# Out-projection with 128 tokens per matmul, and attention weights kept on chip, in a four-layer scan and attention kernel

## The chip, the cores and the metric

The kernel runs on one core of a Trainium2 chip. The metric is the device time of one execution in microseconds (us), the median of the runs shown. The core has five instruction streams that run beside each other and wait for each other by semaphores: PE (matrix products), DVE and POOL (elementwise work), ACT (elementwise functions and copies) and SP. SP here only issues DMA transfers, all of them, from one queue in order.

## What is computed

The input `x` is 4 images of 64 x 64 tokens with 96 channels. Four layers follow each other:

- layer 0 is a selective-scan block on the normalized image. Tokens are projected to an inner width (192), convolved with a 3 x 3 depthwise filter, scanned in four directions with 16 states per channel (`h = h * exp(dt * A) + dt * u * B`, `y = sum(h * C)`), normalized, multiplied by a gate `silu(z)`, projected back to 96 channels and added to `x`;
- layer 1 does the same in the frequency domain: a real two-dimensional FFT gives 33 x 64 frequencies, real and imaginary parts make 192 channels, the inner width is 384, and after the out-projection (384 to 192 channels) the inverse FFT is added to its input;
- layers 2 and 3 are an attention without softmax, whose value for all tokens can be had from one small product `x^T x`, and a feed-forward network quantized to 8-bit floats.

```
y = _layernorm(y, out_norm_w, out_norm_b)
y = y * jax.nn.silu(z)
return y @ out_proj_w.T        # layer 1: [64 x 33 tokens, 384] @ [384, 192]
```

## The kernel before

**Stages.** `build` runs a head, a long scan stage and a tail. The head (`alone(head, begin0, 0)`) normalizes and projects the first two images of layer 0 with nothing beside it; the task is `normalized` and then `Block.project`. The scan stage (`scans`) goes through six phases: two for layer 0 (two images each) and four for layer 1 (one image each). The tail (`alone(tail, end1, 3)`) finishes image 3: out-projection, inverse FFT, layers 2 and 3.

**Scan steps.** A phase takes four directions, each cut into segments of tokens (eight of 512 for layer 0; 512, 512, 384, 384 and 320 for layer 1). A segment has 12 steps: four quarters of the 16 states times three groups of 128 channels. So there are 2 x 384 + 4 x 240 = 1728 steps. In a step, ACT makes the decay factors (L682), PE transposes the inputs into PSUM (L678), DVE runs four scans (L710), POOL makes the other inputs (L700) and multiplies by C (L747), and PE adds up over the states (L757). The broadcast rows of B and C come by DMA (L624), B and C of a quarter being fetched about three steps ahead into two buffers each.

**Side tasks.** What isn't scan work is written as Python generators that are stepped from three places in every scan step (`slot`). `RATES` gives how many yields of the side tasks a step may take: 2.82 in the layer 1 phases. A yield can ask for a certain place (`LATE`, `BURST`). The side tasks queue up over phases: the phases of images 1, 2 and 3 are given `end1` of images 0, 1 and 2, and `begin1` (FFT, input projection and gate) of all images comes before. When a side task ends, the next one starts; after the last one the remaining scan steps have nothing beside them. In the scan stage the order on PE, DVE, ACT and POOL is the order in which the program is written out, while that of SP's transfers comes from the planner of the framework, as does that of all engines in head and tail. With `E.wide` over 1 (head and tail) up to three such workers are interleaved.

**`end1`, where most of the edit lies.** `Block.gated` goes over the rows of frequencies in blocks of 8, 8, 6, 6 and 5 rows of 64 tokens (in the tail three workers: blocks 0 and 3, 1 and 4, and 2). It loads the scan outputs (`yt`, L403 and L407; `ut`, L409) and the gate (`zb`, L423), transposes and sums them, normalizes, applies the gate (L481 in the tail) and calls the out-projection `out1`. That takes one row of 64 tokens per matmul: `y[:, c, ...]` (128 channels x 64 tokens) is the stationary operand, `wo[:, c, :]` (128 x 192) the moving one, three channel groups are summed in PSUM (L1019), two rows go to ACT in one copy (L1026), and one transfer per block stores them in `att` (L1028), which lies as [64, 33, 192] in DRAM. An f32 matmul shows as two instructions.

`inverse` then loads `ih`, `iw` (L1098, L1100) and `att` in three channel groups of 32 (`at`, L1106), and does two sets of matmuls (L1117, L1133). `tokens` runs layers 2 and 3. It loads the attention weights of a layer with `weights` (L1207): in the scan stage those of layer 2 at its start and those of layer 3 when it comes to it; in the tail those of both layers, and `end1` takes its first yield (`next(rest)`) ahead of `inverse`, so that these eight loads stand ahead of `inverse`'s own on SP. The feed-forward weights are quantized once, in the side task `quantized` of the first phase, and kept.

**Inputs of the projections.** The class `Inputs` prefetches the weights `wi` (L145) and the token tiles `xi` (L150) for `project` (half 0) and `gate` (half 1). `wi` holds both halves, of which `in_proj` (L210) uses one.

Of the kernel before, what the change touches and what calls it, by code (L numbers as in the profile page):

```python
# [7 lines left out]
F32 = mybir.dt.float32  # L8
# [10 lines left out]
NB, HH, WW, CH = 4, 64, 64, 96  # L19
# [3 lines left out]
C, P = 3, 128  # L23
# [7 lines left out]
class Cfg:  # L31
# [5 lines left out]
    def __init__(self, pre, NI, KI, NR, nat, R, parts, rows, segs, eps):  # L37
        self.pre = pre
        self.NI, self.PI, self.KI = NI, P // NI, KI
        self.DI = C * self.PI  # L40
        self.NR, self.L, self.nat = NR, NR * 64, nat
        self.R, self.M = R, R + 2 * NST
        self.parts = parts
        self.rows = [(sum(rows[:i]), n) for i, n in enumerate(rows)]
        self.segs = [(sum(segs[:i]), n) for i, n in enumerate(segs)]
        self.eps = eps
# [66 lines left out]
def together(tasks, width):  # L113

    tasks, active = list(tasks), []
    while tasks or active:
        while tasks and len(active) < width:
            active.append(tasks.pop(0))
        for task in list(active):
            try:  # L120
                yield next(task)
            except StopIteration:
                active.remove(task)


class Inputs:


    def __init__(self, blk, sp, xf, chunks, half, nm, w):
        self.blk, self.sp, self.xf, self.half, self.nm, self.w = blk, sp, xf, half, nm, w  # L130
        self.todo = [
            (c, r, n) for c in chunks for p0, p1 in blk.cfg.parts for r, n in blk.rows_of(p0, p1, half == 0)
        ]
        self.ahead, self.wi = [], {}
        for _ in range(2):
            self.load()

    def load(self):
        if not self.todo:
            return  # L140
        sp, cfg, nc = self.sp, self.blk.cfg, self.blk.nc
        c, r, n = self.todo.pop(0)
        if c not in self.wi:
            t = sp.tile([CH, cfg.KI, 2, cfg.PI], F32, name=f"{cfg.pre}_wi_{self.nm}_{c}", tag=f"wi{self.w}", bufs=2)
            nc.sync.dma_start(out=t, in_=self.blk.w["inw"][:, :, :, c, :])  # L145
            self.wi[c] = t
        x = sp.tile(
            [CH, 2, 512], F32, name=f"xi{self.half}_{self.nm}_{c}_{len(self.todo)}", tag=f"xin{self.w}", bufs=3
        )
        nc.sync.dma_start(out=x[:, :, : n * 64], in_=self.xf[:, :, r * 64 : (r + n) * 64])  # L150
        self.ahead.append((self.wi[c], x))
# [6 lines left out]
class Block:  # L158


    def __init__(self, tc, pool, cfg, w, ident, dram):
# [4 lines left out]
        def load(name, shape, src=None):  # L166
            t = pool.tile(list(shape), F32, name=f"{cfg.pre}_{name}", tag=f"{cfg.pre}{name}")
            nc.sync.dma_start(out=t, in_=w[name] if src is None else src)
            return t

        self.xpw = load("xpw", (P, C, 4, cfg.NI * cfg.M))
        self.dtw = load("dtw", (cfg.NI * cfg.M, 4, C * P))
        self.dtb = load("dtb", (P, C, 4))
# [29 lines left out]
    def in_proj(self, out, wi, half, xin, n):  # L203

        cfg = self.cfg
        for i in range(cfg.NI):
            for ki in range(cfg.KI):
                if i or ki:
                    yield
                self.nc.tensor.matmul(  # L210
                    out[i * cfg.PI : (i + 1) * cfg.PI, :n],
                    wi[:, ki, half, :],
                    xin[:, max(i, ki), :n],
                    start=(ki == 0),
                    stop=(ki == cfg.KI - 1),
                )
# [789 lines left out]
def out1(att, b):  # L1006


    def task(E, blk, sp, wo, y, r, nr, w):
        nc = E.nc  # L1010
        a = sp.tile([HH, 8, 2 * CH], F32, name=f"ab_{b}_{r}", tag=f"ab{w}")
        for i0 in range(0, nr, 2):
            m = min(2, nr - i0)
            po = E.psum(f"po1_{b}_{r}_{i0}")[:HH, : 4 * CH].rearrange("p (k c) -> p k c", k=2)
            for i in range(m):
                if i:
                    yield
                for c in range(C):
                    nc.tensor.matmul(  # L1019
                        po[:, i, :],  # L1020
                        y[:, c, (i0 + i) * HH : (i0 + i + 1) * HH],
                        wo[:, c, :],
                        start=(c == 0),
                        stop=(c == C - 1),
                    )
            E.defer(lambda i0=i0, m=m, po=po: nc.scalar.copy(a[:, i0 : i0 + m, :], po[:, :m, :]))  # L1026
            yield
        nc.sync.dma_start(out=att[:, r : r + nr, :], in_=a[:, :nr, :])  # L1028

    return task  # L1030

# [124 lines left out]
def quantized(E, cp, ins, quant):  # L1156

    nc = E.nc
    shapes = (("w1", [CH, 4 * CH]), ("w2", [P, 3, CH]), ("b1", [P, 3]), ("b2", [P, CH]))
    with E.pool("qw") as sp:  # L1160
        loaded = []
        for ly in (2, 3):
            for name, shape in shapes:
                t = sp.tile(shape, F32, name=f"{name}_{ly}", tag=f"{name}{ly}")
                src = ins[f"l{ly}_{name}"]
                nc.sync.dma_start(out=t, in_=src.to_broadcast([P, CH]) if name == "b2" else src)
                loaded.append((ly, name, shape, t))
        for _ in range(6):
            yield
        for ly, name, shape, t in loaded:  # L1170
            keep = cp if name in ("w1", "w2") else sp
            r = keep.tile(shape, F8, name=f"q{name}_{ly}", tag=f"q{name}{ly}")
            yield LATE
            nc.vector.tensor_copy(r, t, saturate=False)
            if keep is sp:
                r, q = cp.tile(shape, F32, name=f"k{name}_{ly}", tag=f"k{name}{ly}"), r
                nc.vector.tensor_copy(r, q)
            quant[ly][name] = r
    yield


def tokens(E, ins, consts, ident, x1, b, out, quant):
# [4 lines left out]
    nc = E.nc  # L1187
    A, Q, W = CH + 1, 8, E.wide
    with E.pool(f"tk{b}") as sp:
# [7 lines left out]
            nc.scalar.copy(id16, ident)  # L1197
        nc.gpsimd.memset(xn[:, :, CH:A], 1.0)

        def weights(ly):  # L1200

            nm, w, bufs = f"{b}_{ly}", {}, min(W, 2)
            for name, shape in (
                ("wqkv", [A, 3 * CH]), ("wqt", [CH, A]), ("wff", [CH, CH]), ("bff", [A, CH]),
            ):
                t = w[name] = sp.tile(shape, F32, name=f"{name}_{nm}", tag=name, bufs=bufs)
                nc.sync.dma_start(out=t, in_=ins[f"l{ly}_{name}"])  # L1207
            w.update(quant[ly])
            return w

        ws = [weights(ly) for ly in ((2, 3) if W > 1 else (2,))]
        yield
        x = sp.tile([P, NT, CH], F32, name=f"tok_{b}", tag="tok")
        nc.sync.dma_start(out=x, in_=x1.rearrange("(p t) c -> p t c", t=NT))
# [71 lines left out]
        def small(rows, lhs, rhs, name, into):  # L1286

            pw = E.psum(name)[:rows, : rhs.shape[1]]
            nc.tensor.matmul(pw, lhs, rhs, start=True, stop=True)
            E.defer(lambda: into(pw))  # L1290
# [83 lines left out]
            yield from together([layer_norm(f"{b}_2a", p) for p in parts], W)  # L1374
        for ly in (2, 3):
            nm = f"{b}_{ly}"
            if len(ws) < ly - 1:
                ws.append(weights(3))
            q = ws[ly - 2]
            wq = q["wqkv"]  # L1380
            if W == 1:
                yield from norm_all(nm + "a")
            pg = E.psum(f"pg_{nm}")[:A, :A]
            for t in range(NT):
                nc.tensor.matmul(pg, xn[:, t, :], xn[:, t, :], start=(t == 0), stop=(t == NT - 1))  # L1385
                if t % 4 == 3:
                    yield
            gs = sp.tile([A, A], F32, name=f"gs_{nm}", tag="gs")
            nc.scalar.copy(gs, pg)
            yield  # L1390
            gv = sp.tile([A, CH], F32, name=f"gv_{nm}", tag="gv")
            small(A, gs, wq[:, 2 * CH : 3 * CH], f"pgv_{nm}", lambda t: nc.scalar.copy(gv, t))
            yield
            mt = sp.tile([CH, CH], F32, name=f"mt_{nm}", tag="mt")
            small(CH, gv, wq[:, CH : 2 * CH], f"pm_{nm}", lambda t: nc.vector.tensor_tensor(mt, t, mask, ALU.mult))
            yield
            pw = sp.tile([CH, CH], F32, name=f"pws_{nm}", tag="pws")
            small(CH, mt, q["wff"], f"pw_{nm}", lambda t: nc.scalar.copy(pw, t))
            yield
            wo = sp.tile([A, CH], F32, name=f"wo_{nm}", tag="wo")  # L1400
            small(A, q["wqt"], pw, f"pe_{nm}", lambda t: nc.vector.tensor_tensor(wo, t, q["bff"], ALU.add))
            yield
            if W > 1:
                yield from together([part(ly, p, wo, q) for p in parts], W)
                continue
            for g in range(NT // 4):
                yield from attend(nm, g, 0, wo)
            yield from norm_all(nm + "f")
            for g in range(NT // 4):
                yield from feed(nm, g, 0, q)  # L1410
# [212 lines left out]
```

## Time and profile before

| | |
|---|---|
| median of 3 runs | 11260.47 us (11260.01 to 11280.23) |
| the profiled execution | 11260.07 us |
| its span, first to last instruction | 11258.3 us |
| head (to the first L747) | 0 to 221.8 us |
| scan, layer 0 phases | 221.8 to 5135.5 us |
| scan, layer 1 phases | 5135.5 to some 10877 us, 1456, 1413, 1435 and 1434 us |
| tail | some 10877 to 11258.3 us |
| L1019, all images | 792 instructions, first at 7103.6, last at 11018.3 us |
| L1028, stores of `att` | 20, at 445 to 500 ns on SP's queue |
| L1207, attention weights | 8 loads of each of four names, 7548.9 to 11029.7 us |
| feed-forward of images 0, 1, 2 ended (their L1412 store) | 8307.7 us; some 9583; 10842.7 us |

An execution's time is 1.8 us above its span here, for what lies around it. In the lines of the timeline the first number is the start and the second the length, both in us; in brackets stands the time for which the engine sat idle before, and what ended that. SPq is SP's DMA queue: its time is that of issuing a transfer, not of moving the data. PEld are weight loads, which overlap PE's matmuls. An entry of PE stands for an instruction from start to end, so entries overlap, and the spacing of starts tells the rate.

### The profile page before, as it was taken

How to read it: one execution, taken by the hardware profiler on the slowest of the kernel's cores; microseconds unless marked ns; L12 is line 12 of the kernel's file. 1: busy time of each engine (PE TensorE's matmuls, PEld its weight loads, DVE VectorE, ACT ScalarE, POOL GpSimd, SP SyncE). 2: the span in 40 equal slices, each digit the busy share in tenths (PEclk: the TensorE clock that was granted, in tenths of full speed). 3: DMA queues.
4: the chain of work that ended last, by engine and by line, in shares of the span. 5: the costliest groups of instructions: out<-in, count | busy, mean ns of one | idle time of the engine just before them, and what ended most of it. 6: DMA issues, size and time to landing. Idle time of an engine off the chain costs nothing. (4 is left out here: it accounts for less than half of the span.)

```text
span 11258.3 us, 163664 instructions
## 1 busy us (share of the span) xinstructions
PE 9023.4 (80%) x54944; PEld 6618.2 (59%) x54944; DVE 9756.0 (87%) x10419; ACT 9354.2 (83%) x19456; POOL 9614.9 (85%) x7464
## 2 busy tenths in 40 slices
PE   6678788777888888888888888887788777887775
PEld 2555555555667666656665665655556555655554
DVE  6889999889999998999888787988988889789864
ACT  3779999998898998998778788879888888778853
POOL 2999999888998998999789798988989889889860
PEclk8889999888998998999889899998899888899887
DMA  4655554555665556555554444542244322542242
GB/s 146 146 131 128 133 131 120 153 158 143 163 162 134 137 138 144 133 144 161 154 141 131 128 135 137 172 118 92 96 138 143 102 92 98 157 125 96 82 131 40
DMA packets 1205139, 1466.87 MB, mean 130 GB/s; under 512 B 480839, under 2 KB 1017295, under 8 KB 1145799
## 3 DMA queue, kind: packets, MB, share of 16 engines
q1 hardware_dynamic: 1204295, 1456.40, 47.7%
q8 instruction: 434, 7.11, 0.3%
q14 instruction: 410, 3.36, 0.1%
HBM read 1219.66 MB, written 236.50 MB: 129 GB/s over the span
## 5 line engine op out<-in xcount | busy, mean ns | idle before, releaser
L747 POOL TENSOR_TENSOR h_l<-h_l,bc_l 128x1536 f32<-128x1536 f32 (+2 forms) x1728 | 4784.4, 2769 | 192.1 <-DVE h_l L710 73.1
L700 POOL TENSOR_TENSOR h_l<-du_l,bc_l 128x512 f32<-128x512 f32 (+2 forms) x3456 | 3970.4, 1172 | 620.1 <-PE acc_l L757 581.1
L646 ACT ACTIVATE bx_l<-dut_l,bt_l 128x192 f32<-128x192 f32 (+2 forms) x6272 | 2754.6, 499 | 0.3
L757 PE MATMUL acc_l<-ident,h_l 128*128 128x128 f32 (+1 forms) x16656 | 2430.6, 299 | 243.5 <-POOL h_l L747 242.1
L757 PEld LDWEIGHTS acc_l<-ident,h_l 128*128 128x128 f32 (+1 forms) x16656 | 2130.9, 154 | 836.8 <-POOL h_l L747 384.9
L682 ACT ACTIVATE ax_l<-delta_l,l_alog 128x512 f32<-128x512 f32 (+2 forms) x3456 | 2140.7, 667 | 0.0
L710 DVE TENSOR_TENSOR_SCAN h_l<-b_l,state_l,h_l 128x512 f32<-128x512 f32 (+2 forms) x1388 | 1507.6, 1109 | 123.1 <-ACT b_l L682 104.5
L678 PE MATMUL b_l<-ident,bx_l 128*128 128x128 f32 (+1 forms) x6886 | 1215.4, 295 | 210.2 <-DVE h_l L710 203.2
L678 PEld LDWEIGHTS b_l<-ident,bx_l 128*128 128x128 f32 (+1 forms) x6886 | 854.6, 149 | 816.6 <-DVE h_l L710 464.4
L682 ACT ACTIVATE b_l<-delta_l,l_alog 128x512 f32<-128x512 f32 (+2 forms) x1970 | 1232.6, 626 | 117.2 <-DVE h_l L710 49.4
L710 DVE TENSOR_TENSOR_SCAN b_l<-ax_l,state_l,b_l 128x512 f32<-128x512 f32 (+2 forms) x853 | 967.5, 1134 | 254.8 <-PE b_l L678 253.6
L678 PE MATMUL ab_l<-ident,bx_l 128*128 128x128 f32 x5312 | 896.1, 298 | 223.1 <-DVE h_l L710 213.2
L710 DVE TENSOR_TENSOR_SCAN h_l<-ab_l,state_l,h_l 128x512 f32<-128x512 f32 x803 | 992.7, 1261 | 83.2 <-ACT ab_l L682 48.8
L682 ACT ACTIVATE ab_l<-delta_l,l_alog 128x512 f32<-128x512 f32 x1326 | 912.8, 688 | 152.3 <-DVE h_l L710 81.4
L757 PE MATMUL acc_l<-ident,k_l 128*128 128x128 f32 x4760 | 785.8, 293 | 294.8 <-DVE k_l L728 281.6
L710 DVE TENSOR_TENSOR_SCAN h_l<-ax_l,state_l,b_l 128x512 f32<-128x512 f32 (+2 forms) x853 | 963.2, 1129 | 65.0 <-PE b_l L678 62.7
L678 PEld LDWEIGHTS ab_l<-ident,bx_l 128*128 128x128 f32 x5312 | 654.2, 151 | 583.4 <-DVE h_l L710 414.9
L728 DVE TENSOR_TENSOR k_l<-b_l,bc_l 128x512 f32<-128x512 f32 (+2 forms) x1344 | 832.2, 619 | 47.2 <-DMA bc_l<-l_xd_l 1.0
L297 PE MATMUL pc_l<-pad_l,l_dg 128*128 128x512 f32 (+2 forms) x1656 | 788.1, 564 | 59.5 <-ACT uh_l L275 46.8
L757 PE MATMUL acc_l<-ident,hk_l 128*128 128x128 f32 x3628 | 591.8, 297 | 293.7 <-DVE hk_l L728 280.8
L757 PEld LDWEIGHTS acc_l<-ident,k_l 128*128 128x128 f32 x4760 | 582.8, 150 | 390.7 <-DVE k_l L728 317.9
L710 DVE TENSOR_TENSOR_SCAN ab_l<-ax_l,state_l,ab_l 128x512 f32<-128x512 f32 x496 | 631.9, 1274 | 114.5 <-PE ab_l L678 113.8
(252 smaller groups left out, 14452.2 us busy)
## 6 DMA issues: line engine op xcount, KB each, us to landing
bc_l<-l_xd_l SPq DMA_DIRECT2D x640, 512.0 KB
bc_l<-l_xd_l SPq DMA_DIRECT2D x512, 256.0 KB
bc_l<-l_xd_l SPq DMA_DIRECT2D x128, 1024.0 KB
bc_l<-l_xd_l SPq DMA_DIRECT2D x128, 768.0 KB
us_l<-l_u SPq DMA_DIRECT2D x96, 768.0 KB
l_y<-y_l SPq DMA_DIRECT2D x288, 256.0 KB
yt_l<-l_y SPq DMA_DIRECT2D x264, 192.0 KB
yt_l<-l_y SPq DMA_DIRECT2D x128, 384.0 KB
```

The costliest lines, as they stand in the source:

```text
L297: nc.tensor.matmul(pc[:, : n * 64].rearrange("p (r w) -> p r w", w=64), diag[:, t, :], pad[:, r - p0 + dy : r - p0 + dy + n, dx : dx + 64] ...
L646: nc.scalar.activation(t[:n, b, :, ch], z.dut[:n, b, :, ch], AF.Copy, scale=z.bt[:n, b, m : m + 1])
L678: nc.tensor.transpose(pb[:, t : t + n], st.z.bx[st.q, j][:n, b, st.c], ident[:n, :n])
L682: nc.scalar.activation(out, z.delta[:, st.c, : z.S], AF.Exp, scale=z.blk.A[:, st.c, z.k, n : n + 1])
L700: nc.gpsimd.tensor_tensor(st.h[:, 1 + j, :S], st.z.du[:, st.c, :S], st.z.b[st.q][:, j, :S], ALU.mult)
L710: nc.vector.tensor_tensor_scan(h[:, ::step], a[:, ::step], b[:, ::step], 0.0 if z.first else z.state[st.c][:, n : n + 1], ALU.mult, ALU.add,)
L728: nc.vector.tensor_tensor(hk[:, : z.S], kept_at(st, j), z.c[st.q][:, j, : z.S], ALU.mult)
L747: nc.gpsimd.tensor_tensor(h, h, z.c[st.q][:, 1 : 1 + m, : z.S], ALU.mult)
L757: nc.tensor.matmul(z.acc[st.c][:m, b, :], hc[:, t : t + m], ident, start=(first and b == 0), stop=(last and b == 0), is_transpose=True,)
```

## The change

Four edits:

- `out1` takes pairs of rows, 128 tokens per matmul, so the result has 128 partitions: the even row of a pair in partitions 0 to 63, the odd one in 64 to 127. A block of 8, 6 or 5 rows makes 4, 3 or 3 tiles (the last of 5 with 64 tokens). One copy takes two tiles; a single row has a copy of its own. `att` gets two stores per block, one for the even and one for the odd rows, and a third where a row is single.
- The number of yields of `out1` goes with the tiles: 17 an image, where it was 33.
- The attention weights of layers 2 and 3 are loaded in `quantized` into the pool that lives as long as the program; `weights` and its loads go.
- `Inputs` loads the half of `wi` that is used, and makes `xin` tiles as long as its longest block.

```diff
@@ Inputs
-        self.ahead, self.wi = [], {}
+        self.ahead, self.wi, self.most = [], {}, 64 * max(n for _, _, n in self.todo)
...
-            t = sp.tile([CH, cfg.KI, 2, cfg.PI], F32, ..., tag=f"wi{self.w}", bufs=2)
-            nc.sync.dma_start(out=t, in_=self.blk.w["inw"][:, :, :, c, :])
+            t = sp.tile([CH, cfg.KI, cfg.PI], F32, ..., tag=f"wi{self.w}", bufs=2)
+            nc.sync.dma_start(out=t, in_=self.blk.w["inw"][:, :, self.half, c, :])
...
-            [CH, 2, 512], F32, ..., tag=f"xin{self.w}", bufs=3
+            [CH, 2, self.most], F32, ..., tag=f"xin{self.w}", bufs=3
@@ in_proj
-                    wi[:, ki, half, :],
+                    wi[:, ki, :],
@@ out1
-        a = sp.tile([HH, 8, 2 * CH], F32, name=f"ab_{b}_{r}", tag=f"ab{w}")
-        for i0 in range(0, nr, 2):
-            m = min(2, nr - i0)
-            po = E.psum(f"po1_{b}_{r}_{i0}")[:HH, : 4 * CH].rearrange("p (k c) -> p k c", k=2)
+        a = sp.tile([P, 4, 2 * CH], F32, name=f"ab_{b}_{r}", tag=f"ab{w}")
+        pairs = nr // 2
+        for i0 in range(0, (nr + 1) // 2, 2):
+            m = min(2, (nr + 1) // 2 - i0)
+            po = E.psum(f"po1_{b}_{r}_{i0}")[:, : 4 * CH].rearrange("p (k c) -> p k c", k=2)
             for i in range(m):
+                t, n = (i0 + i) * P, P if i0 + i < pairs else HH
                 if i:
                     yield
                 for c in range(C):
                     nc.tensor.matmul(
-                        po[:, i, :],
-                        y[:, c, (i0 + i) * HH : (i0 + i + 1) * HH],
-                        wo[:, c, :],
-                        start=(c == 0),
-                        stop=(c == C - 1),
+                        po[:n, i, :], y[:, c, t : t + n], wo[:, c, :], start=(c == 0), stop=(c == C - 1)
                     )
-            E.defer(lambda i0=i0, m=m, po=po: nc.scalar.copy(a[:, i0 : i0 + m, :], po[:, :m, :]))
-            yield
-        nc.sync.dma_start(out=att[:, r : r + nr, :], in_=a[:, :nr, :])
+
+            def put(i0=i0, m=m, po=po):
+                full = min(m, pairs - i0)
+                if full > 0:
+                    nc.scalar.copy(a[:, i0 : i0 + full, :], po[:, :full, :])
+                if full < m:
+                    nc.scalar.copy(a[:HH, pairs : pairs + 1, :], po[:HH, full : full + 1, :])
+
+            E.defer(put)
+            yield
+        v = att[:, r : r + 2 * pairs, :].rearrange("h (k o) c -> o h k c", o=2)
+        for o in range(2):
+            nc.sync.dma_start(out=v[o], in_=a[o * HH : (o + 1) * HH, :pairs, :])
+        if nr % 2:
+            nc.sync.dma_start(out=att[:, r + nr - 1, :], in_=a[:HH, pairs, :])
@@ quantized
+    A = CH + 1
...
+    for ly in (2, 3):
+        for name, shape in (("wqkv", [A, 3 * CH]), ("wqt", [CH, A]), ("wff", [CH, CH]), ("bff", [A, CH])):
+            t = quant[ly][name] = cp.tile(shape, F32, name=f"{name}_{ly}", tag=f"{name}{ly}")
+            nc.sync.dma_start(out=t, in_=ins[f"l{ly}_{name}"])
@@ tokens
-        def weights(ly):
...
-                t = w[name] = sp.tile(shape, F32, name=f"{name}_{nm}", tag=name, bufs=bufs)
-                nc.sync.dma_start(out=t, in_=ins[f"l{ly}_{name}"])
...
-        ws = [weights(ly) for ly in ((2, 3) if W > 1 else (2,))]
...
-            if len(ws) < ly - 1:
-                ws.append(weights(3))
-            q = ws[ly - 2]
+            q = quant[ly]
```

More of the change, by code (lines that the diff above doesn't have):

```diff
@@ L143, in load @@
         if c not in self.wi:
-            t = sp.tile([CH, cfg.KI, 2, cfg.PI], F32, name=f"{cfg.pre}_wi_{self.nm}_{c}", tag=f"wi{self.w}", bufs=2)
-            nc.sync.dma_start(out=t, in_=self.blk.w["inw"][:, :, :, c, :])
+            t = sp.tile([CH, cfg.KI, cfg.PI], F32, name=f"{cfg.pre}_wi_{self.nm}_{c}", tag=f"wi{self.w}", bufs=2)
+            nc.sync.dma_start(out=t, in_=self.blk.w["inw"][:, :, self.half, c, :])
             self.wi[c] = t
         x = sp.tile(
-            [CH, 2, 512], F32, name=f"xi{self.half}_{self.nm}_{c}_{len(self.todo)}", tag=f"xin{self.w}", bufs=3
+            [CH, 2, self.most], F32, name=f"xi{self.half}_{self.nm}_{c}_{len(self.todo)}", tag=f"xin{self.w}", bufs=3
         )
@@ L1198, in tokens @@
         nc.gpsimd.memset(xn[:, :, CH:A], 1.0)
-        def weights(ly):
[L1202 to L1205, printed above, removed]
-                t = w[name] = sp.tile(shape, F32, name=f"{name}_{nm}", tag=name, bufs=bufs)
-                nc.sync.dma_start(out=t, in_=ins[f"l{ly}_{name}"])
-            w.update(quant[ly])
-            return w
-        ws = [weights(ly) for ly in ((2, 3) if W > 1 else (2,))]
         yield
```

## The prediction

> **What bounds the kernel now.** I read the page first, then the chain that ended last, then the timeline around its pieces, then counts per stretch.
>
> ```profile
> PE 9023.4 (80%) x54944; PEld 6618.2 (59%) x54944; DVE 9756.0 (87%) x10419; ACT 9354.2 (83%) x19456; POOL 9614.9 (85%) x7464
> ```
>
> No engine is full. From 222 to 10877 us the program is a chain of 1728 scan steps in which DVE, ACT, POOL and PE hand tiles to each other, while the side tasks fill gaps at up to 2.82 yields a step. Before (0 to 222 us) and after (10877 to 11258 us) stand a head and a tail in which little overlaps. The edit touches a few percent of the work, so the question is in which of the three stretches it lies on the path.
>
> The chain that ended last, start and length in us:
>
> ```profile
> 10957.66 17.15 PE po L1019 x104
> ...
> 11005.97 12.66 PE po L1019 x66
> 11022.75 4.53 SPq L1207
> 11027.32 1.84 SPq L1207
> 11030.01 3.71 SPq L1098
> ...
> 11042.12 6.27 DMA at<-att
> 11048.52 20.36 PE piv L1117 x320
> ...
> 11119.77 3.55 PE pao L1301 x32
> ```
>
> So in the tail (image 3) both passes of the out-projection (L1019) and the weight loads on SP's queue (L1207) are themselves the path. The timeline gives the speeds and SP's order:
>
> ```profile
> 10966.08 0.47 ACT L1026 COPY ab<-po 64x384 f32<-64x384 f32 x1 [2.45 <-PE po L1019]
> ...
> 10969.98 0.47 ACT L1026 COPY ab<-po 64x384 f32<-64x384 f32 x1 [2.45 <-PE po L1019]
> ...
> 11020.30 0.73 SPq L1207 DMA_DIRECT2D wqkv<-in_l_wqkv  x1
> ...
> 11029.67 0.29 SPq L1207 DMA_DIRECT2D bff<-in_l_bff  x1
> ...
> 11034.25 9.67 SPq L1106 DMA_DIRECT2D at<-att  x6
> ```
>
> Two evictions that follow each other like this have 24 matmul instructions between them (two workers, two tiles each, three channel groups, two instructions per f32 matmul): 3.90 / 24 = 0.163 us an instruction. L1019's mean of 359 ns is latency; the spacing is what counts. SP issues eight weight loads from 11020.30 to 11029.96, and the loads of `at`, which the inverse transform needs, stand behind them.
>
> In the scan, POOL's product (L747) runs once a step. Stretches of the last phase at segment length 512, with and without side work:
>
> ```profile
> 10736.20:10842.50 106.30, 50.86 (x16) 0.92 0.27 90
> 10842.60:10864.90 22.30, 12.69 (x4) 0.88 0.31 118
> ```
>
> The page has no step times, so this count per stretch gives them.
>
> **What the Trainium skill says.** "TensorE: Matmul & The Clock Gate", step-by-step: a matmul's time follows the columns of the moving operand, the weight load that of the stationary one, and the load of the next tile runs under the current matmul. The trace agrees: L1301, 128 stationary and 96 moving columns, runs 32 in 3.55 us, 0.111 us each, so 128 stationary columns fit under 0.163 us. "DMA: Bandwidth & Descriptors", on why a DMA increments its semaphore by 16: a transfer from SP's queue uses the largest number up to 16 of DMA engines that divides its slowest dimension; 96 partitions get 16, a prime number gets one. `wqkv` and `bff` have 97. The trace agrees: around 11024 to 11034 packets of 1152 bytes run at 21 to 25 a microsecond in a row, 97 of them in about 4.5 us. The same page, on the anatomy of a DMA: completion waits for the write receipt, an estimate of 2 us; the trace's att packets end some 2 us after their issue.
>
> **Tail.** (a) 198 instructions of L1019 become 102 for the image: the first pass (blocks of 8, 8, 6 rows) 132 -> 66, the second (6 and 5 rows) 66 -> 36. In the first, worker 2 comes early and then PE waits for DVE until 10957.66; behind that the chain counts 104 instructions, workers 0 and 1's 96 and the rest of worker 2's, in 17.15 us. Now 48 are left there, worker 2's 18 being done before: 48 x 0.163 = 7.8 us, gain 9.3 (8.7 if four more slip behind). The second: 30 fewer x 0.163 = 4.9, its starting waits for DVE (1.9 us) staying. The next transposes, the last `yt` loads and all after shift with them. Six stores now leave SP where three did, at 0.49 us each, done before the `yt` loads can go. (b) Eight L1207 issues go: 11020.30 to 11030.01, 9.7 us. What is late next: the `at` loads wait for the stores of `att`. Five stores instead of two stand before them, 0.49 us each, of which only about 0.6 us follows the last eviction; then mask, `ih`, `iw` (1.5 us), and about 2 us of landing. With PE's 14.2 us gone the last eviction ends at 11019.1 - 14.2 = 11004.9, the last store lands near 11007.6, and `at` starts there instead of at 11034.25: 26.6 us. SP's 3.71 us at `ih`, a queueing delay behind the weights, is in this. Tail: -26 (bounds -12, if L1019 gains nothing, and -29).
>
> **Head.** The built program puts the four weight loads of layer 2 directly ahead of the first `wi` and `xi` loads, and layer 3's 32 issues later, after the prefetches.
>
> ```profile
> 51.81 0.72 SPq L145 DMA_DIRECT2D l_wi<-in_l_inw  x1
> 54.15 1.22 SPq L150 DMA_DIRECT2D xi<-xn  x2
> ...
> 58.08 1.76 PE L210 MATMUL pi_l<-xi,l_wi 96*64 96x448 f32 x4 [34.56 <-DMA xi<-xn]
> ```
>
> PE stands idle 34.56 us for `xi`. Issue: 0.73 + 0.72 + 0.42 + 0.39 = 2.3 us, of which 1.6 hides in the pause before 54.15. But 97 rows of `wqkv` (4.5 us) and of `bff` (by its bytes and the smaller rows some 2.7) sit on one DMA engine, on which a sixteenth of each `xi` load follows. `xi` then lands near 62: +4 (bounds 0 and +8). The convolution behind it is limited by PE and DVE, so this stays. Layer 3's loads come when the next inputs are already there: 0. Halved `wi` loads: 0, since `xi` lands after them; smaller `xin` buffers move waits, and the waits that I see added in the instruction order (PE before the gate's second `xi`, DVE before the first pad memset) are for work long done: 0.
>
> **Scan.** Images 0 to 2 do their out-projection as side work, 33 yields each, now 17. A built program's order tells where the side work of each image ends: 5, 11 and 16 steps earlier. So 16 more steps at the very end (length 512) are free of it: 106.30 / 16 = 6.64 us against 22.30 / 4 = 5.58, 16 x 1.07 = 17 us. Earlier, out-projection steps give way to the work behind: stretches of 12 steps at length 384 take 64.7 to 67.6 us with out-projection in them and 60 to 68, on average 64, with the feed-forward: 0.2 a step on 16 steps, 3 us. Sum -20. Bounds: 0 (another engine takes the time back), and -47, 3 x 96 x 0.163, were PE the limit throughout. Seven evictions fewer an image (0.47 us, ACT) lie inside. The L1207 loads taken out here (24 of about 0.45 us) had nobody waiting: 0; SP instead gets 6 more att stores an image, in front of later broadcast loads, covered by their being fetched three steps ahead.
>
> **Sum.** +4 - 20 - 26 = -42 from the profiled execution's 11260.07 us (span 11258.3, about 2 around it), which is the median, 11260.47: **11218 us**. A measurement of this kernel tells about 0.2% (22.5 us) from no change.
>
> **Rivals.** (1) The three terms as above: 11218, its own range 11205 to 11232; 0.55. (2) The scan gives nothing, DVE and POOL (87, 85%) setting the step: 11238; for it, PE's 80%; against it, the step without side work, 5.58 us where 6.64 was; 0.17. (3) PE limits the scan: 11191; for it, POOL's longest wait on PE is at L700, 581.1 us; against, the side-free PE time is not all gained; 0.17. (4) Not what it says: 128 stationary columns double the matmul's time. Then the tail keeps 12, the scan nothing: 11252; against it L1301; 0.06. (5) Slower: the att stores, 33 instead of 15 in the three phases, each waiting on SP for ACT's copy, hold up the broadcast loads behind them. To end above 11283 it has to take back 42 + 22.5 = 64 us, so it decides from 64 / 33 = 1.9 us lost per store, after the three steps (some 17 us) by which the loads run ahead; SP mostly waits for POOL to free those buffers, which speaks against; 0.05, say 11290.
>
> **Numbers.** Faster: all of (1) but 0.02, (3), half of (2): 0.79; the same: 0.02, the other half of (2) and (4), 0.16; slower 0.05. The range runs from (3) to between (2) and (4): 11190 to 11246.
>
> **What would show it.** L1019 down to 408 instructions at the same 0.163 spacing, its tail passes about 7.8 and 7.8 us; no weight issue after 1 ms; `at` issued some 11 us after the second pass began rather than 28.3; PE's first L210 near 62 us; the last L1356 of the scan about 16 steps before its end, at 5.6 us a step after it; everything between the head and 7100 us shifted by a constant. It would be wrong if `at` waits longer for the 768-byte att rows, or if the steps with fewer side yields don't shorten.

## The result

The changed kernel takes 11178.47 us (median of 5 runs, 11174.47 to 11198.16), the kernel before, on the same chip, 11274.52 us (5 runs, 11260.01 to 11280.23). The medians differ by 96 us; by the ratio of the runs, 0.9922 with a 95% interval of 0.9911 to 0.9933, it is some 88 us less. The forecast was 11218 us, 42 less than the 11260.47 that it started from (the median of the first three runs before); the measured time lies below its range. The profiled execution of the changed kernel took 11196.25 us (span 11194.5), one of its two longer ones.

In what follows "before" and "after" are the two profiled executions. The start of POOL's product (L747, once a step) cuts each into stretches. "Three phases" are the last three of layer 1 (steps 1008 to 1727), those that have the out-projection of images 0, 1 and 2 as side work.

| us | before | after | difference |
|---|---|---|---|
| head, to the first L747 | 221.8 | 227.2 | +5.4 |
| two layer 0 phases | 4913.7 | 4914.7 | +1.0 |
| first layer 1 phase (no out-projection in it) | 1456.4 | 1468.2 | +11.8 |
| three phases | 4281.8 | 4225.1 | -56.7 |
| tail, from the last L747 | 384.7 | 359.4 | -25.3 |

The page's line of busy times:

```profile
PE 8922.4 (80%) x54560; PEld 6578.7 (59%) x54560; DVE 9751.5 (87%) x10419; ACT 9340.7 (83%) x19428; POOL 9616.7 (86%) x7464
```

PE has 384 instructions and 101 us less; the shares look as before, and don't tell where the time went. The tail of after, chain that ended last (start, length):

```profile
10918.78 7.46 PE po L1021 x44
...
10959.52 7.97 PE po L1021 x36
...
10978.28 6.43 DMA at<-att
10984.85 20.23 PE piv L1127 x320
```

The two passes of the out-projection take 7.46 and 7.97 us, where they took 17.15 and 12.66. What follows, the landing of `at` and the first products of the inverse, has its old length (6.43 and 20.23). SP's part of the same place, from the timeline:

```profile
10968.61 0.56 SPq L1038 DMA_DIRECT2D att<-ab  x1
...
10969.89 0.38 SPq L1108 DMA_DIRECT2D ih<-in_ih  x1
10970.32 0.42 SPq L1110 DMA_DIRECT2D iw<-in_iw  x1
10970.92 9.21 SPq L1116 DMA_DIRECT2D at<-att  x6
```

No weight load stands between the last store of `att` and the loads of `at`, which begin 11.4 us after the second pass did (28.3 before). The head, timeline:

```profile
51.18 0.29 SPq L1174 DMA_DIRECT2D wqkv<-in_l_wqkv  x1
51.52 1.38 SPq L1174 DMA_DIRECT2D wqt<-in_l_wqt  x1
52.95 0.42 SPq L1174 DMA_DIRECT2D wff<-in_l_wff  x1
53.41 0.31 SPq L1174 DMA_DIRECT2D bff<-in_l_bff  x1
53.76 4.40 SPq L145 DMA_DIRECT2D l_wi<-in_l_inw  x1
58.29 1.31 SPq L150 DMA_DIRECT2D xi<-xn  x2
...
63.15 1.76 PE L210 MATMUL pi_l<-xi,l_wi 96*64 96x448 f32 x4 [40.09 <-DMA xi<-xn]
```

PE's first product comes at 63.15 us instead of 58.08; the issue of `l_wi`, 0.72 us before, takes 4.40 behind the weights. So head and tail came out as forecast in size. Of the -64 us of the two profiled executions, and of the -88 us by the ratio, the scan is the part that isn't accounted for: -20 was forecast, and the three phases alone gave -57.

### The profile page after: what moved, and what is told of

It reads as the page before. It is cut to its first block, busy times and chain, and to the rows that moved or that the text cites. A ratio compares the mean times of both kernels' runs of the same rounds, so it can differ in the third digit from the quotient of the medians.

```text
span 11194.5 us, 162858 instructions
## 1 busy us (share of the span) xinstructions
PE 8922.4 (80%) x54560; PEld 6578.7 (59%) x54560; DVE 9751.5 (87%) x10419; ACT 9340.7 (83%) x19428; POOL 9616.7 (86%) x7464
## 4 chain that ended last, share of the span: by engine, by line
POOL 31%; PE 23%; ACT 20%; DVE 16%; issue 7%; DMA 2%; SPq 1%; POOLq 0%; DVEq 0%; ACTq 0%
POOL h_l L747 14%; POOL h_l L700 12%; DVE h_l L710 7%; PE acc_l L757 6%; ACT bx_l L646 4%; ACT ax_l L682 4%; ACT b_l L682 3%; DVE b_l L710 2%; DVE ab_l L710 2%; PE b_l L678 2%; PE pc_l L297 2%; POOL du_l L604 2%; PE pp_l L571 1%; PE pi_l L210 1%; ACT ab_l L682 1%
## 5 line engine op out<-in xcount | busy, mean ns | idle before, releaser
L747 POOL TENSOR_TENSOR h_l<-h_l,bc_l 128x1536 f32<-128x1536 f32 (+2 forms) x1728 | 4783.3, 2768 | 176.1 <-DVE h_l L710 56.1
```

What stands on the lines that cost most here:

```text
L747: nc.gpsimd.tensor_tensor(h, h, z.c[st.q][:, 1 : 1 + m, : z.S], ALU.mult)
```

## Experiments

Theory A, the prediction's: the scan gains because the side work is shorter, 17 yields of the out-projection instead of 33, and the halved matmul work as such gives nothing there. Theory B, its third rival: in the steps that hold the out-projection PE sets the pace, and 3 x 96 instructions of 0.163 us fewer are 47 us. Kernels e1 to e4 separate instructions from yields, e5 measures the instructions alone, e6 and e7 the head, e8 to e12 the place of the side work. Ratios are to the kernel before, run beside each. Stretches come from one profile of each kernel. The four profiles that have the changed kernel's out-projection, yields and rate (after, e1, e6, e7) lie between 4216.6 and 4225.1 us in the three phases and between 357.1 and 361.2 in the tail, so differences under some 9 and 4 us between two profiles tell nothing.

**e1: the changed kernel again.**

> The changed kernel once more, as the yardstick of the other runs of this set and to see how steady its stretches are. Head (to the first L747) 227, that is +5 on before; scan (first to last L747) -44 on before in the one profiled pair, in which a drift of +12 us in the first layer 1 phase, where the edit has nothing to do, is included: if that drift is an accident of the execution, the scan is near -60 here; tail -25. Total 80 to 98 below before.

Measured: 11180.6 us, ratio 0.9925 (0.9912 to 0.9937). Head 225.4, layer 0 4902.7, first layer 1 phase 1465.2, three phases 4216.6, tail 357.1. The result repeats.

**e2: only the kept weights and the halved input weights.** `out1` is the old one.

> Only the kept weights and the halved input weights; the out-projection with 64 tokens per matmul and 33 yields as before. Theory of the prediction: head +5 (first L747 near 227), scan 0 within 5 us, tail -10 to -13 (eight issues of 9.7 us and some landing less, PE's two passes as before): total -5 to -8. Rival: the kept weights or the smaller input buffers change the scan themselves; then part of the -44 to -60 us shows here.

Measured: 11251.64 us, ratio 0.9987 (0.9981 to 0.9994). Head 224.0, three phases 4277.6 (4281.8 before), tail 376.5 (384.7). The scan phases with the out-projection don't notice the kept weights and the halved input weights by more than profiles differ.

**e3: 128 tokens per matmul, but 33 yields.**

```
                 if i:
                     yield
+                if n == P:
+                    yield
                 for c in range(C):
```

> The changed kernel with an empty yield ahead of every tile of 128 tokens, so that the out-projection takes 33 yields of an image again while its matmul work stays halved. Theory A (the scan gains because the side tasks take 48 yields fewer, and steps at the end of the scan run without side work): scan back to -3 to +3 of before, tail -25, head +5, total near -20. Theory B (PE's time is what the scan waits for in the steps with the out-projection: 3 x 96 instructions at 0.163 us = 47 us): scan stays 40 to 60 below before, total -65 to -90. Both in part: in between.

Measured: 11201.83 us, ratio 0.9941 (0.9928 to 0.9953). Three phases 4232.9, that is -44.7 against e2, with the side work in the same steps as in e2. In the steps that hold the out-projection of images 0, 1 and 2 (1100 to 1152, 1312 to 1364, 1524 to 1575) it is 16.7, 6.4 and 17.9 us shorter than e2, 41 of the 45. Away from the out-projection the two run alike: steps 1176 to 1187 take 64.5 us and steps 1188 to 1199 71.1 us in both. In the steps with the out-projection they differ. Steps 1524 to 1571 (image 2), busy time in the stretch, first of e2, then of e3; columns are stretch, length, then PE, PEld, DVE, ACT, POOL with instructions, PE's clock, DMA share, GB/s:

```profile
9669.60:9933.60 264.00, 232.30 (x1403) 167.90 (x1403) 213.44 (x283) 209.00 (x452) 209.51 (x193) 0.92 0.48 136
```

```profile
9648.00:9896.10 248.10, 216.08 (x1322) 162.89 (x1322) 211.77 (x283) 207.29 (x447) 209.57 (x193) 0.91 0.51 145
```

PE's busy time falls by 16.2 us and the stretch by 15.9. PE's idle time is 31.7 us in one and 32.0 in the other, while that of DVE and POOL shrinks by 14 and 16 us. The stretch follows PE's work, though PE is busy 88% and not 100%. The chain that ended last agrees: in this stretch of e2 the products of the out-projection make up 12.3% of it (32 us) and PE as a whole 136 of 264 us; in e3 they make up 3.7% (9 us) and PE 99 of 248. So PE sets the pace here in the sense that its instructions lie on the path for half of the stretch; ACT, DVE and POOL hold most of the rest, and no run took work from them in these steps. Theory A, which expected the scan back at its old length, falls as the whole account.

**e4: 64 tokens per matmul, but 17 yields**: the yield between the two rows of a tile is taken out of the old `out1`; weights kept.

```
             for i in range(m):
-                if i:
-                    yield
                 for c in range(C):
```

> Weights kept, the old matmuls with 64 tokens, but two rows of them between two yields, so 17 yields an image: the changed kernel's schedule with the old kernel's PE work, in lumps of 12 instructions (2 us). Theory A (fewer yields): scan -20 to -60, tail -12, head +5, total -27 to -67. Theory B (PE's work): scan 0, or above it for the lumps, total -7 or more.

Measured: 11235.77 us, ratio 0.9975 (0.9968 to 0.9983). Three phases 4265.3, that is -12.3 against e2; by phase -5.8, +6.7 and -13.2. Tail 372.0. So the shorter schedule gives little without the halved work, not much more than profiles differ.

**e5: every matmul of the changed kernel twice.**

```
-                    nc.tensor.matmul(
-                        po[:n, i, :], y[:, c, t : t + n], wo[:, c, :], start=(c == 0), stop=(c == C - 1)
-                    )
+                    for twice in range(2):
+                        nc.tensor.matmul(
+                            po[:n, i, :], y[:, c, t : t + n], wo[:, c, :],
+                            start=(c == 0 and twice == 0), stop=(c == C - 1 and twice == 1),
+                        )
```

> The changed kernel (17 yields, same copies, same stores, kept weights) with every matmul of the out-projection issued twice into the same sum: 204 instructions an image instead of 102 (before had 198). The out-projection's result is twice what it should be; nothing is left out. Theory B (PE sets the pace of the scan steps in which the out-projection runs; fewer copies, other stores and the shape of the result are worth nothing): the three phases with out-projection return to what the kept weights with 64 tokens and 17 yields gave, some 4265 us where the changed kernel has 4217 to 4225, that is +40 to +48, and the tail +13 to +15; total +53 to +63 on the changed kernel, ratio to before near 0.9975. Rival (the gain came from the seven copies fewer on ACT, the different stores, or the shorter wait for the finished tile): scan phases stay near 4220.

Measured: 11242.14 us, ratio 0.9969 (0.9958 to 0.998). Three phases 4265.0, where e4 with the same yields and 198 instructions an image has 4265.3; tail 378.7 (6.7 above e4's; the runs don't show why). Taken together, the copies, stores and result shapes of the changed kernel are worth nothing in the three phases that shows; the number of its PE instructions accounts for the gain. Steps 1512 to 1559 of e4, e5 and e7 (e7 has the out-projection of the changed kernel), columns as above:

```profile
9590.50:9858.70 268.20, 234.04 (x1448) 174.27 (x1445) 219.63 (x295) 215.81 (x464) 210.17 (x194) 0.94 0.46 138
```

```profile
9620.10:9889.50 269.40, 236.44 (x1454) 185.15 (x1454) 219.40 (x295) 212.98 (x457) 210.21 (x194) 0.92 0.47 138
```

```profile
9571.70:9823.80 252.10, 217.80 (x1351) 166.76 (x1352) 219.51 (x295) 212.61 (x457) 210.28 (x193) 0.93 0.49 146
```

PE's idle time is 34.2, 33.0 and 34.3 us again. In the chain that ended last the out-projection's products have 33 and 37 us of these stretches in e4 and e5, and 21 in e7. And e5's tail says what one instruction costs (chain that ended last):

```profile
10961.98 21.45 PE po L1022 x132
11018.22 13.73 PE po L1022 x72
```

21.45 / 132 = 0.163 us with 128 stationary columns, the same as 0.163 with 64 before.

**e6: the 97-row weights loaded as 96 rows and 1 row.**

```
+            n = shape[0] // CH * CH
-            nc.sync.dma_start(out=t, in_=ins[f"l{ly}_{name}"])
+            nc.sync.dma_start(out=t[:n], in_=ins[f"l{ly}_{name}"][:n])
+            if n < shape[0]:
+                nc.sync.dma_start(out=t[n:], in_=ins[f"l{ly}_{name}"][n:])
```

> The changed kernel with the loads of the 97-row weights cut into 96 rows and 1 row. If the head's +4 to +5 comes from 97 rows being moved by one DMA engine, on which a part of each input tile then waits, the first L210 comes at 60 us or earlier instead of 63.15, and the first L747 2 to 4 us earlier (head 222 to 225). Rival (it comes from SP's time to issue four more loads ahead of the inputs): no gain, rather +1 for the added issues. Scan and tail unchanged; total within 5 us of the changed kernel either way.

Measured: 11181.81 us, ratio 0.9919 (0.9906 to 0.9931). Head 221.2. Timeline of e6:

```profile
50.81 0.83 SPq L1175 DMA_DIRECT2D wqkv<-in_l_wqkv  x1
51.69 0.29 SPq L1177 DMA_DIRECT2D wqkv<-in_l_wqkv  x1
...
52.84 0.42 SPq L145 DMA_DIRECT2D l_wi<-in_l_inw  x1
53.59 1.31 SPq L150 DMA_DIRECT2D xi<-xn  x2
...
57.75 1.76 PE L210 MATMUL pi_l<-xi,l_wi 96*64 96x448 f32 x4 [34.60 <-DMA xi<-xn]
```

The issue of `l_wi` is back from 4.40 to 0.42 us, and PE starts at 57.75, even a little before the 58.08 of the kernel without these loads, although four weight loads still stand ahead (`bff` of layer 2 went behind the inputs here, so its part isn't separated). The DMA packets show what changed: the 97 rows of layer 2's `wqkv`, 1152 bytes each, start one after the other from 53.29 to 58.36 us in after, and all between 52.49 and 53.46 in e6. Of the 96 rows of `wqt`, issued behind them, 90 go at once in after and six, a sixteenth, only at about 58 us; the issue of `l_wi` ends at 58.16. So the head's loss was the 97 rows, not SP's time to issue the four loads. In the total 5 us can't be told from none.

**e7: loads behind the first input loads, at 11 us, and cut as in e6.**

> As the run with 96 and 1 rows, and the loads of the kept weights are also issued right behind the first loads of the input image (about 11 us), where SP waits for other engines anyway, instead of ahead of the first input tiles of the projection. Expected: the first L210 near 58 us as in the kernel before, head 221 to 223, total 3 to 6 us below the changed kernel. Rival: the eight loads delay the constants behind them on SP and the head stays at 225 to 227.

Measured: 11179.19 us, ratio 0.9921 (0.9908 to 0.9934). Head 223.5, the first L210 at 60.02. It is not better than e6: the twelve issues push back the constants and then the stores of `xn`, whose last issue starts its run at 47.01 instead of 44.49 in e6.

**e8 to e12: another rate.** e7 with 2.75, 2.9, 3.0, 2.80 and 2.84 yields a step in the four layer 1 phases, instead of 2.82.

```
-RATES = [1.6, 2.35, 2.82, 2.82, 2.82, 2.82]
+RATES = [1.6, 2.35, 2.75, 2.75, 2.75, 2.75]
```

> As the run before, with 2.75 instead of 2.82 yields of side tasks a step in the four layer 1 phases, so that the side work spreads over some of the 23 steps at the end that now have none. If PE's (and the other engines') time per step is used evenly, spreading work thinner gains what is lost at the end, 0 within 5 us; if the crowded steps wait for one engine and steps with spare time take some of that work, it gains 5 to 15 us; if the side work then reaches past the last step, it loses.

> As e7, with 2.9 instead of 2.82 yields a step in the layer 1 phases. The lower rate cost 45 us, and the side work then ended at the last step instead of 23 steps before it. If a step with side work costs a fixed amount whatever it holds, the side work now ends some 40 steps before the end and the scan gains some 15 to 20 us more; if the crowded steps are set by PE and the rate only moves work, 0 within 5 us; if the lower rate lost by the places where its work fell against the segments, this rate may as well lose.

> As e9, with 3.0 yields a step. Fixed cost of a step with side work: 35 to 45 us below e7, since the side work ends some 65 steps before the end. PE sets the crowded steps: 0 within 5 us of e7, or slower. A change whose sign isn't that of the rate's (e9 and e10 on different sides of e7) would say that the places decide.

> As e7, with 2.80 yields a step. This and the next run ask how much the place of the side work alone is worth, since 0.02 yields a step move it by no more than 12 steps at the end of the scan. If the 12 to 16 us that the runs with 17 instead of 33 yields gained come from the side work being shorter, such small shifts change the three phases with out-projection (4220 us in e7) by less than 8 us, upward here by about 3. If the place decides, they swing by 10 us or more, and the gain of the fewer yields can't be told from it.

> As e7, with 2.84 yields a step. Side work shorter: the three phases within 8 us of e7's 4220, about 3 lower. Place decides: 10 us or more away, in either direction.

| yields a step | time, us | ratio (95%) | three phases, us |
|---|---|---|---|
| 2.75 (e8) | 11226.1 | 0.9962 (0.995 to 0.9974) | 4255.0 |
| 2.80 (e11) | 11211.77 | 0.9939 (0.9923 to 0.9956) | 4240.8 |
| 2.82 (e7) | 11179.19 | 0.9921 (0.9908 to 0.9934) | 4220.1 |
| 2.84 (e12) | 11206.17 | 0.9935 (0.992 to 0.995) | 4255.7 |
| 2.90 (e9) | 11241.19 | 0.9977 (0.9967 to 0.9987) | 4270.2 |
| 3.00 (e10) | 11297.7 | 1.0026 (1.0018 to 1.0034) | 4310.2 |

Both directions lose, and 0.02 yields a step move the three phases by 21 and 36 us, always upward, against 8 expected if only the length of the side work counted. The rate holds in the first layer 1 phase too, which took 1463.1 us in e7, 1470.7 in e11 and 1441.2 in e12: over all four phases it is +28 and +14, where the four profiles at 2.82 (after, e1, e6, e7) lie within 16. So the loss with 2.84 is less sure than that with 2.80. (With 2.75 the side work reaches past the scan: the last feed-forward store comes 12 us behind the last L747, and the tail has 368.7 us.) As far as single profiles tell, where each piece of side work falls against the scan steps weighs more here than how long it is in all. What makes a place good wasn't found, and the 12 us that e4 gained over e2 (and the 13 by which the four profiles of the changed kernel's out-projection lie below e3) can't be split into shorter work and luckier places. The 45 us for the instructions don't suffer from this: they were measured twice between kernels with equal yields (e2 and e3; e4 or e5 and the changed kernel).

No run was better than the changed kernel by more than the measurement can tell; e6 repairs its head at no cost that shows.

## Why the prediction was right and wrong

**Head: right in size and in its cause, not in the path.** +4 forecast, first L210 near 62; +5.4 and 63.15 measured. The cause was given as one DMA engine for 97 rows ("DMA: Bandwidth & Descriptors" of the Trainium skill, on why a DMA increments its semaphore by 16: the largest number up to 16 that divides the slowest dimension). The trace agrees: 97 rows one after the other for 5.1 us, and six rows of the next load behind them. But the prediction let a sixteenth of each `xi` load wait behind the rows; in after, SP's queue itself stood at the issue of `l_wi`, so `xi` was issued 4.1 us later (58.29 instead of 54.15), and only 0.9 us came on top of that.

**Tail: right.** -26 forecast, -25.3 measured. The passes were to take 7.8 and 7.8 us and took 7.46 and 7.97; `at` was to start 11 us into the second pass and did at 11.4. By parts: the kernels with the old amount of PE work and kept weights (e2, e4, e5) have a mean tail of 375.7 us, those with the new (after, e1, e3, e6, e7) 360.0, so PE gave 15.7 (forecast 14.2); e2 and e4 have on average 10.5 us less than before, so the weights gave that (forecast 12.4). The two errors, 1.5 and 1.9 us, cancel; they are no larger than profiles differ. That 128 stationary columns might double the matmul is out (0.163 us in both).

**Scan: wrong, and in a certain step.** The sum was 17 for the end, 3 for the earlier steps, and nothing for the instructions, with 47 as a mere bound ("were PE the limit throughout").

- *The instructions: 45 us instead of 0.* This is the failed step: the prediction held that halving PE's work in the out-projection steps would not shorten them. It took the busy shares of the whole span (PE 80%, DVE 87%, POOL 85%) and concluded that PE doesn't set the step. It held stretches with out-projection against stretches with feed-forward, 0.2 us a step apart, and put the difference down as the whole worth of the edit; but that compares two kinds of side work, not one kind at full and at half the matmuls. The chain that ended last couldn't tell: in the profile of before it begins at 10872.38 us, so it says nothing of the scan. A view that pointed the right way was at hand: busy time by stretch, asked of all engines in the steps concerned. Before, steps 1524 to 1571 with the out-projection, then a stretch some 500 us later with norms of layer 2 and scan work:

```profile
9660.10:9926.80 266.70, 234.26 (x1403) 169.90 (x1403) 213.25 (x283) 208.85 (x452) 209.37 (x192) 0.92 0.49 135
```

```profile
10174.00:10310.00 136.00, 97.16 (x635) 75.31 (x635) 130.41 (x134) 122.73 (x248) 125.03 (x90) 0.91 0.27 91
```

  In the first PE is the busiest engine, 88% against 80 and 79 for DVE and POOL; in the second it has 71% and DVE 96. The 80% of the whole is an average over such stretches. "Perfetto Trace Analysis" of the Trainium skill ("Identifying the Most-Contended Engine") says to optimize the engine with the highest occupancy, but to judge PE by its share of peak arithmetic and by the busy time of its weight loads, not by matmul busy time. Here the weight loads were at 64% in that stretch and by themselves would have ranked PE last (the share of peak arithmetic wasn't worked out); the matmul share in the stretch is what pointed to the engine that e3 and e5 show to set the pace.

- *The end of the scan: 6 to 9 us instead of 17.* The side work did end about where it was said to (in step 1705), and the steps behind it did get shorter, but not to 5.58 us. After, steps 1704 to 1715, all but the first two without side work, busy times as above:

```profile
10700.20:10775.80 75.60, 50.85 (x335) 39.41 (x333) 70.23 (x67) 62.07 (x115) 74.64 (x53) 0.93 0.32 112
```

  That is 6.30 us a step, with POOL busy for 74.64 of 75.60, and the chain that ended last on POOL for 73 of them: POOL sets this pace. The 5.58 came from the last four steps of the scan, which are short of POOL work, since little is left to prepare for steps to come. Those four in the kernel before, all engines:

```profile
10842.60:10864.90 22.30, 14.67 (x90) 11.49 (x89) 22.13 (x22) 12.43 (x21) 22.30 (x13) 0.88 0.31 118
```

  13 POOL instructions in 4 steps there, 53 in 12 above; L747 (3.17 us a step in both) apart, POOL has 2.4 us a step in the last four (22.30 / 4 less 3.17), and 3.05 in the stretch above (74.64 / 12 less 3.17). Steps 1704 to 1727 took 143.5 us before and 141.2 in e2, 134.9 after: 6 to 9 us. The sample was too small and not typical of a step.

- *The earlier steps: 3 forecast, some 3 to 7 left over* (12 to 13 for the yields less the 6 to 9 of the end), within what the place of the side work alone does (e11, e12).

Together: 45 + 13 = 58 us for the scan's three phases by the experiments, 57 to 65 by after and e1; 20 forecast. The rival "PE limits the scan" had the right mechanism, and its 47 the right size; it was given 0.17 and taken as an alternative to the shorter side work, while the two add up. With the forecast's own head and tail, +4 - 58 - 26 = -80, where the ratio says -88 and the two profiles -64. That the profiles show less is mostly the first layer 1 phase, below.

**The marker "everything up to 7100 us shifted by a constant"** did not hold: the first layer 1 phase was 11.8 us longer after. The edit does reach into it, since `begin1` loads its inputs there with the halved `wi` and the smaller `xin` buffers; that the edit has nothing to do there, as e1's expectation has it, doesn't hold. All kernels with that edit at this rate took longer than the 1456.4 of before, but they differ among themselves by as much, without an edit in this phase that tells them apart: 1458.0 (e4), 1459.9 (e6), 1466.9 (e3) and 1470.5 us (e2). With one profile of before, a cost of the input edit is neither shown nor excluded.

**The slower rival** (stores holding up broadcast loads) found nothing to stand on: e5 has the changed kernel's stores and the same time in the three phases as e4, which has the old ones, 4265.0 and 4265.3. That a loss by the stores is offset by the seven copies fewer an image wasn't tested apart.

## What to carry to other kernels

Ask for the busy time of all engines in the very stretch that holds the edited work: an engine with 80% of the whole can set the pace there, and here the work taken from it came back almost in full (45 us of 47), though it was at 88% and not at 100%. When an edit has two effects (less work, fewer slots), ask whether they add up before choosing between them; here they did. Take the price of a step from steps with full pipelines, not from the last ones of a loop, and expect a hand-placed schedule to answer to a small shift of its side work: the two shifts of 0.02 yields a step cost 21 and 36 us in the three phases, though a part of the second came back in the phase before.

## What was not expected of the hardware

- PE at 88% busy set the pace of the steps with the out-projection: its idle time stayed at 32 us in 264 and in 248 us (e2, e3) and at 33 to 34 us in e4, e5 and e7, while its work changed by 16 to 19 us.
- A weight load of 97 rows took 5.1 us from its first row to its last and held the issue of a later load on SP's queue for 4.40 us; cut into 96 rows and 1, its rows took 1.0 us and the same issue 0.42.
- A change of 0.7% in the rate at which side work is mixed in (2.82 to 2.80 or 2.84) cost 21 and 36 us in the three phases of single profiles, 28 and 14 in all four phases of layer 1, and by the ratios (0.9939 and 0.9935 against 0.9921, with intervals that overlap) some 20 and 16 us of the whole.
